# Half loads completed by ScalarE copies, two shifts replaced by loads, and the products for M placed earlier in a fused CIN kernel

## The chip, the cores and the metric

The kernel runs on one core of a Trainium2 chip. The metric is the device time of one execution in microseconds (us), lower is better; where a profile is shown, its times count from the start of the profiled span. The engines are called PE (TensorE), ACT (ScalarE), DVE (VectorE), POOL (GpSimd) and SP (SyncE, which here only issues DMAs); PEld is PE's loading of weights.

## The reference

The reference is a three-layer "compressed interaction network" on `x` of shape (1024, 64, 16): batch, fields, embedding. Each layer multiplies every field of `x` with every field of the last hidden state, elementwise over the embedding, and contracts the 64 x 64 products with a weight matrix of 128 rows.

```python
x0 = x; h = x; xs = []
for i in range(3):
    z = jnp.einsum('bfe,bge->bfge', x0, h)          # all pairs of fields
    z = z.reshape(Bn, f0 * fh, e)
    y = jnp.einsum('oc,bce->boe', Ws[i], z) + bs[i][None, :, None]
    if i != 2: x_i, h = y[:, :64], y[:, 64:]         # half goes out, half goes on
    else:      x_i, h = y, y
    xs.append(x_i)
pooled = jnp.sum(jnp.concatenate(xs, axis=1), axis=2)
return pooled @ fc_w.T + fc_b                        # (1024, 1)
```

All data are float32. Since the result is one number per batch row, the last layer's weights can be folded with `fc_w` into one 64 x 64 x 64 form, called M in this text, that acts on pairs of hidden and input fields.

## The kernel before, in words

The batch is cut into 32 chunks of 32 rows; a chunk is a matrix of 64 fields by N = 512 columns. The products of all field pairs are symmetric, so the kernel forms 16 blocks per chunk, `t = 4*j + i`. Block (j, i) multiplies a copy of x whose rows are rotated by i with a copy rotated by 4(j + 1), and by 16 more in the upper 64 partitions. The first copy is the tile `xa`, of 128 partitions by 4 x 512; its upper 64 partitions hold the same values as its lower 64, since the host array `xra` repeats x's rows with period 64. The second copy is made of four quarters `xb[c][j]` of 128 x 512. `product(c, j)` (line 242) multiplies a whole `xa` with one quarter into a block buffer `z` of 128 x 2048, on DVE by default, on POOL where `engine=nc.gpsimd` says so. `half_contract(c, j)` (line 252) contracts the four blocks of one j on PE into the accumulator `acc`: eight matmuls, two for each block. `w_all` holds the weights; `h1_weights(j)` (line 302) makes its left half from the loaded `w0t` with the help of a copy by ACT (lines 312 and 321 to 326).

This work concerns the head of the kernel, about the first 57 us, in which the first four chunks `c0, c1, c2, c3` (`HEAD`, chunks 2, 3, 0, 1) go through the first layer while the weights for the rest are made. Its order is written out by hand: each engine runs its instructions in the order in which the code names them, and waits at each for its operands and for its output buffer.

- Loads, all on SP's queue, in this order: first row block of c0's `xa`, the first quarter of w0 (`wh`), c0's other blocks, c1's first block, the rest of w0 (`w0r`), the rest of c1's `xa`, w2 in two parts, w1, then c2's `xa` and its four quarters. c3 follows after c0's last product, in c0's `xa` buffer.
- The quarters of c0 and c1 are not loaded. PE makes them out of `xa` with a shift matrix (`shift_pair`, line 221), into PSUM banks. One of each chunk is copied to SBUF by ACT (lines 314 and 339), because POOL multiplies with it.
- Quarters of c2 and c3 are loaded. Where POOL works at the same time, ACT copies a quarter into a PSUM bank first, and DVE reads it there (lines 397 and 429).
- M: `pv` (line 359) on PE, two transposes (line 364) and two small copies (line 371) on DVE, two small copies on ACT (line 372), which together give the weights `v2t`; then `pm` (line 386) on PE, its evacuation by ACT (line 400), a write to memory (lines 415 to 421) and skewed reads back (lines 459 and 465), from which DVE makes the right half of `w_all` (line 495).
- After c3 PE runs the second half of the head's contractions with that right half (`head_q_tile`, line 270); then the steady loop begins, whose instructions are sorted by due times written by hand (line 526 is its matmul helper, lines 634 and 651 its products and sums, line 554 its copies into PSUM).

PSUM tiles come from three tags: `acc` with four banks, `y` and `set` with two each. A tile of a tag waits until the tile that had its bank before is done with. The pool of `xa` has three buffers, that of `xb` nine.

Of the kernel before, what the change touches and what calls it, by code (L numbers as in the profile page):

```python
# [37 lines left out]
F32 = mybir.dt.float32  # L38
# [4 lines left out]
F = 64  # L43
# [3 lines left out]
N = CB * E  # L47
# [3 lines left out]
NI = 4  # L51
NJ = 4
NT = NI * NJ
XR = 128 + NI
# [16 lines left out]
def cin_kernel(ctx, tc, xra, xrb, wh, w0r, w1h, w2t, wx1, wx0, vec, out):  # L71
    nc = tc.nc
    ctx.enter_context(tc.manual_schedule())
    const = ctx.enter_context(tc.tile_pool(name="const", bufs=1))
    xp = ctx.enter_context(tc.tile_pool(name="xp", bufs=3))
    sp = ctx.enter_context(tc.tile_pool(name="sp", bufs=2))
    ps = ctx.enter_context(tc.tile_pool(name="ps", bufs=2, space=bass.MemoryType.PSUM))
    dr = ctx.enter_context(tc.tile_pool(name="dr", bufs=1, space=bass.MemoryType.DRAM))
    halves = [slice(0, F), slice(F, 128)]

    def const_tile(name, shape):
        return const.tile(shape, F32, tag=name, name=name)
# [4 lines left out]
    def take(uses=1):  # L87
        n = vacant.pop(0)
        left[n] = uses
        return n  # L90

    def used(n, times=1):
        left[n] -= times
        assert left[n] >= 0
        if left[n] == 0:
            vacant.append(n)
# [22 lines left out]
    for base in (0, 64, -64):  # L119
        nc.gpsimd.affine_select(  # L120
            out=shift, in_=shift, compare_op=ALU.not_equal, fill=1.0, base=base,
# [19 lines left out]
    xas, xbs, xxs, es = {}, {}, {}, {}  # L141

    def load_xa(c, at=slice(0, NI)):
        if c not in xas or at.start == 0:
            xas[c] = xp.tile([128, NI, N], F32, tag="xa", name=f"xa_{c}")
        nc.sync.dma_start(  # L146
            out=xas[c][:, at, :],
            in_=bass.AP(
                tensor=xra.tensor, offset=c * XR * N + at.start * N,
                ap=[[N, 128], [1, (at.stop - at.start) * N]],  # L150
            ),
        )

    def quarter(c, j):
        xbs.setdefault(c, {})[j] = xp.tile([128, N], F32, tag="xb", name=f"xb_{c}_{j}", bufs=9)
        return xbs[c][j]

    def load_xb(c, *js):
        for j in js or range(NJ):
            nc.sync.dma_start(out=quarter(c, j), in_=xrb[c, :, j, :])  # L160
# [22 lines left out]
    def load_chunk(c):  # L183
        load_xa(c)
        load_xb(c)

    c0, c1, c2, c3 = HEAD
# [5 lines left out]
    w1s = flat(w1b)  # L193
    load_xa(c0, slice(0, 1))
    nc.sync.dma_start(out=w0t[:, 0, :], in_=wh)
    load_xa(c0, slice(1, 2))
    load_xa(c0, slice(2, 4))
    load_xa(c1, slice(0, 1))
    nc.sync.dma_start(out=w0t[:, 1:NJ, :], in_=w0r)
    load_xa(c1, slice(1, 4))  # L200
    w0s = [w0t[:, j, :].rearrange("p (i v g) -> p i v g", v=2, g=F) for j in range(NJ)]
    xb_gps = [quarter("gps", n) for n in range(2)]
    for k in range(2):
        nc.sync.dma_start(out=w2s[k], in_=w2t[k])
    nc.sync.dma_start(out=w1s, in_=w1h)
    load_xa(c2)
    load_xb(c2)


# [2 lines left out]
    def shifted(c, j, tag):  # L212
        xbs.setdefault(c, {})[j] = ps.tile(
            [128, N], F32, tag=tag, name=f"xp_{c}_{j}", bufs=4 if tag == "acc" else 2
        )

    def shift_pair(c, js):
        for r, j in enumerate(js):
            for h in range(2):
                at = 4 * (j + 1) + 16 * h  # L220
                nc.tensor.matmul(  # L221
                    xbs[c][j][halves[h]], shift[halves[r], at : at + F],
                    xas[c][halves[r], 0, :], start=True, stop=True,
                )
# [6 lines left out]
    acc = const_tile("acc", [128, 2, NCH // 2, CB])  # L231
# [3 lines left out]
    def new_acc(c, n=N, tag="acc"):  # L235
        accs[c] = ps.tile([128, n], F32, tag=tag, name=f"acc_{c}", bufs=4 if tag == "acc" else 2)

    def product(c, j, first=0, last=NI, engine=nc.vector, uses=1):
        if first == 0:
            zs[c, j] = take(uses)  # L240
        at = slice(first, last)
        engine.tensor_tensor(  # L242
            blocks[zs[c, j]][:, at, :], xas[c][:, at, :],
            xbs[c][j].unsqueeze(1).to_broadcast([128, last - first, N]), ALU.mult,
        )

    def half_contract(c, *js, last=None):
        for j in js:
            for i in range(NI):
                t = j * NI + i  # L250
                for n in range(2):
                    nc.tensor.matmul(  # L252
                        accs[c][halves[n]], w_all[:, t, 0:64],
                        blocks[zs[c, j]][:, i, n * H2 : (n + 1) * H2],
                        start=(t == 0), stop=(j == last and i == NI - 1),
                    )
            used(zs[c, j])

    def keep_h1(c):
        for n in range(2):  # L260
            nc.scalar.activation(
                hb[halves[c % 2], c // 2, n * H2 : (n + 1) * H2], accs[c][halves[n]],
                AF.Identity, bias=bh1[halves[n]],
            )
# [36 lines left out]
    def h1_weights(j, other=None):  # L301
        nc.vector.tensor_tensor(
            w_all[:, j * NI : (j + 1) * NI, 0:64], w0s[j][:, :, 0, :],
            w0s[j][:, :, 1, :] if other is None else other, ALU.add,
        )
# [5 lines left out]
    w0o = [w0p[:, 0], w0p[:, 1], w0q[:, 0], w0q[:, 1]]  # L311
    nc.scalar.copy(w0o[0], w0s[0][:, :, 1, :])
    h1_weights(0, w0o[0])
    nc.scalar.copy(xb_gps[0], xbs[c0][1])
    xbs[c0][1] = xb_gps[0]
    for i in ((0, 2), (2, 3), (3, 4)):
        product(c0, 1, *i, engine=nc.gpsimd)
    product(c0, 0, 0, 1)
    product(c0, 0, 1, 2)
    product(c0, 0, 2, NI)  # L320
    nc.scalar.copy(w0o[1], w0s[1][:, :, 1, :])
    product(c0, 2, 0, 2)
    h1_weights(1, w0o[1])
# [6 lines left out]
    half_contract(c0, 0)  # L330


    for j, tag in ((0, "y"), (3, "acc"), (1, "y"), (2, "set")):
        shifted(c1, j, tag)
    shift_pair(c1, (0, 3))
    half_contract(c0, 1)
    shift_pair(c1, (1, 2))
    new_acc(c1, H2)
    nc.scalar.copy(xb_gps[1], xbs[c1][3])
    xbs[c1][3] = xb_gps[1]  # L340

    product(c0, 3)
    load_chunk(c3)
    half_contract(c0, 2, 3, last=3)
    keep_h1(c0)


    for j in range(NJ - 1):
        product(c1, j)
    product(c1, NJ - 1, engine=nc.gpsimd)  # L350

# [17 lines left out]
    for h in range(2):  # L369
        at = slice(32 * h, 32 * h + 32)  # L370
        nc.vector.tensor_copy(v2t[halves[h], at], v2q[halves[h]])
        nc.scalar.copy(v2t[halves[1 - h], at], v2q[halves[h]])
    used(v2b)
    half_contract(c1, 0, 3, 1)


    mb = take()
# [15 lines left out]
    pcx = ps.tile([128, 1], F32, tag="acc", name="pcx", bufs=4)  # L393
    for to in halves:
        nc.tensor.matmul(pcx[to], v2t[0:64], bh2, start=True, stop=True)
    xb2 = ps.tile([128, N], F32, tag="set", name=f"xp_{c2}_{NJ - 1}")
    nc.scalar.copy(xb2, xbs[c2][NJ - 1])
    xbs[c2][NJ - 1] = xb2
    for m in (0, 2, 1, 3):
        nc.scalar.copy(m_sb[:, m, :], pms[m])  # L400

    half_contract(c1, 2, last=2)

# [3 lines left out]
    def m_ap(f1, f2, dims):  # L409
        return bass.AP(tensor=md.tensor, offset=md.offset + f1 * row + f2 * F, ap=dims)  # L410
# [3 lines left out]
    for half, queue in enumerate((nc.sync, nc.scalar)):  # L414
        queue.dma_start(
            out=m_ap(0, 32 * half, [[row, F], [1, 32 * F]]), in_=m_rows[halves[half]]
# [5 lines left out]
        out=m_ap(64, 68, [[row, 4], [4 * F, 7], [1, 4 * F]]),  # L422
        in_=m_rows[0:4, 4 * F :].rearrange("p (k c) -> p k c", c=4 * F),
    )
    used(mb)

    for j in (0, 1):
        xb3 = ps.tile([128, N], F32, tag="y", name=f"xp_{c3}_{j}")
        nc.scalar.copy(xb3, xbs[c3][j])
        xbs[c3][j] = xb3  # L430
    nc.scalar.activation(cx, pcx, AF.Identity, scale=1.0 / QS)
    keep_h1(c1)
    for c in KEPT:
        copy_x(c)

# [567 lines left out]
    last = cuts[1]  # L1003
# [84 lines left out]
```

## Time and profile before

| | us |
|---|---|
| median of 3 runs | 452.6 (452.0 to 452.67) |
| the profiled execution, its own time | 453.01 |
| its span in the profile | 451.2 |
| PE busy in the span | 445.1 |
| DVE busy | 393.1 |
| POOL busy | 364.4 |
| ACT busy | 116.8 |

The times of the stages named in the text come from the profiled execution. A busy share is a mean over stages: which engine matters in a stage is read from who waits for whom there. In the listings of groups and of the timeline a line reads: start and length in us (or count and mean), engine, source line, operation, output from input with sizes, and in brackets the idle time before it and what ended it. Matmuls of float32 leave two records each, so eight matmuls appear as x16.

### The profile page before, as it was taken

The numbers are of one execution on the slowest core, as the hardware profiler recorded it, in microseconds if no ns is written. First come the engines' busy times: TensorE is split into PE (matmuls) and PEld (weight loads), VectorE is DVE, ScalarE is ACT, GpSimd is POOL, SyncE is SP. The second block draws the span as 40 slices with busy tenths as digits, with TensorE's granted clock in tenths as the row PEclk, the third lists the DMA queues.
The fourth block names the chain that finished last, engine by engine and source line by source line (L and its number), as shares of the span: only waits on it lengthen the run. The fifth ranks groups of instructions, "written<-read, shape, count | busy, mean of one in ns | idle before, by whom it ended". The sixth has DMA issues, their size and how long they took to land.

```text
span 451.2 us, 6067 instructions
## 1 busy us (share of the span) xinstructions
PE 445.1 (99%) x2302; PEld 178.9 (40%) x2302; DVE 393.1 (87%) x284; ACT 116.8 (26%) x215; POOL 364.4 (81%) x125
## 2 busy tenths in 40 slices
PE   7999999999999999999999999999999999999997
PEld 4565343442334433343333433344333433344435
DVE  3996598998989998999999899999989999998734
ACT  2163241323312213231221313131131313114111
POOL 5413687999996979899797979979797997979900
PEclk9999999999999999999999999999999999999999
DMA  8996999395949386694958769493967949591500
GB/s 297 415 306 157 322 393 359 114 336 155 324 114 333 121 226 256 133 360 105 281 179 230 259 153 336 107 319 135 252 238 161 341 105 314 176 270 44 107 0 2
DMA packets 34484, 99.67 MB, mean 221 GB/s; under 512 B 6324, under 2 KB 6996, under 8 KB 27864
## 3 DMA queue, kind: packets, MB, share of 16 engines
q1 hardware_dynamic: 31800, 84.70, 52.5%
q0 software_dynamic: 1872, 13.63, 16.9%
q10 hardware_dynamic: 784, 0.95, 0.8%
q8 instruction: 18, 0.29, 0.3%
q14 instruction: 10, 0.08, 0.0%
HBM read 84.00 MB, written 1.64 MB: 190 GB/s over the span
## 4 chain that ended last, share of the span: by engine, by line
PE 96%; DMA 2%; POOL 1%; SPq 0%; issue 0%; DVE 0%; ACT 0%; POOLq 0%; ACTq 0%
PE alpha L526 45%; PE delta L526 20%; PE beta L526 10%; PE acc L526 6%; PE acc L252 6%; PE q L526 3%; PE acc L270 3%; DMA z<-in_w0r 2%; POOL z L651 1%; PE y L526 0%; PE pm L386 0%; PE pv L359 0%; SPq L146 0%; PE xp L221 0%; PE hx L526 0%
## 5 line engine op out<-in xcount | busy, mean ns | idle before, releaser
L651 POOL TENSOR_TENSOR z<-z,z 128x2048 f32<-128x2048 f32 (+1 forms) x78 | 299.6, 3874 | 29.2 <-PE alpha L526 29.1
L634 DVE TENSOR_TENSOR z<-xa,xp 128x2048 f32<-128x2048 f32 x103 | 231.7, 2279 | 2.6 <-issue 1.4
L526 PE MATMUL alpha<-z,ws 128*64 128x512 f32 x624 | 222.1, 593 | 0.0
L526 PEld LDWEIGHTS alpha<-z,ws 128*64 128x64 f32 x624 | 71.7, 137 | 86.3 <-issue 85.5
L526 PE MATMUL delta<-z,w_all 128*64 128x512 f32 x208 | 95.6, 593 | 0.7 <-POOL z L651 0.7
L554 ACT COPY xp<-xb 128x512 f32<-128x512 f32 x88 | 51.6, 588 | 169.5 <-DVE z L634 141.6
L526 PE MATMUL beta<-z,w_all 128*64 128x512 f32 x208 | 93.8, 595 | 0.0
L526 PE MATMUL alpha<-z,w_all 128*64 128x512 f32 x208 | 92.0, 595 | 0.0
L526 PE MATMUL delta<-z,ws 128*64 128x512 f32 x208 | 91.6, 593 | 0.0
L242 DVE TENSOR_TENSOR z<-xa,xp 128x2048 f32<-128x2048 f32 (+2 forms) x23 | 45.0, 2002 | 6.3 <-ACT xp L554 4.8
L242 POOL TENSOR_TENSOR z<-xa,xb 128x2048 f32<-128x2048 f32 x6 | 27.5, 4646 | 19.6 <-DMA xb<-in_xrb 19.6
L526 PEld LDWEIGHTS delta<-z,w_all 128*64 128x64 f32 x208 | 28.3, 137 | 32.9 <-issue 30.4
L526 PEld LDWEIGHTS alpha<-z,w_all 128*64 128x64 f32 x208 | 27.5, 137 | 29.9 <-issue 24.0
L526 PEld LDWEIGHTS delta<-z,ws 128*64 128x64 f32 x208 | 28.1, 137 | 23.7 <-issue 22.8
L526 PEld LDWEIGHTS beta<-z,w_all 128*64 128x64 f32 x208 | 26.9, 137 | 24.2 <-issue 23.0
L252 PE MATMUL acc<-z,w_all 128*64 128x256 f32 x256 | 29.1, 382 | 2.3 <-DVE z L242 2.0
L526 PE MATMUL acc<-z,w_all 128*64 128x512 f32 (+1 forms) x96 | 29.7, 594 | 0.0
L252 PEld LDWEIGHTS acc<-z,w_all 128*64 128x64 f32 x256 | 18.0, 137 | 14.6 <-DVE z L242 3.8
L665 ACT ACTIVATE snap<-alpha,vs 64x512 f32<-64x512 f32 x13 | 8.9, 684 | 54.8 <-PE alpha L526 54.8
L294 DVE TENSOR_REDUCE acc<-uu 128x64 f32<-128x1024 f32 (+2 forms) x19 | 19.6, 1036 | 0.2
L682 DVE SCALAR_TENSOR_TENSOR uu<-alpha,snap 64x512 f32<-64x512 f32 x13 | 9.0, 689 | 12.2 <-PE alpha L526 12.2
L662 ACT COPY snap<-alpha 64x512 f32<-64x512 f32 x13 | 7.6, 581 | 46.2 <-PE alpha L526 29.7
(117 smaller groups left out, 356.4 us busy)
## 6 DMA issues: line engine op xcount, KB each, us to landing
xa<-in_xra SPq DMA_DIRECT2D x32, 1024.0 KB, 8.5
xb<-in_xrb SPq DMA_DIRECT2D x128, 256.0 KB, 8.0
z<-z POOLq DMA_DIRECT2D x13, 1024.0 KB, 8.5
e<-in_xra SPq DMA_DIRECT2D x28, 128.0 KB, 7.3
xx<-in_xra SPq DMA_DIRECT2D x28, 128.0 KB, 2.5
z<-in_w2t SPq DMA_DIRECT2D x2, 1024.0 KB
z<-in_wx SPq DMA_DIRECT2D x2, 1024.0 KB, 10.0
z<-in_w1h SPq DMA_DIRECT2D x1, 1024.0 KB
```

Of the source, the lines that this page charges most:

```text
L242: engine.tensor_tensor(blocks[zs[c, j]][:, at, :], xas[c][:, at, :], xbs[c][j].unsqueeze(1).to_broadcast([128, last - first, N]), ALU.mult,)
L252: nc.tensor.matmul(accs[c][halves[n]], w_all[:, t, 0:64], blocks[zs[c, j]][:, i, n * H2 : (n + 1) * H2], start=(t == 0), stop=(j == last a ...
L270: nc.tensor.matmul(accs[c][halves[1 - c % 2]], w_all[:, t, 64:128], blocks[zs[c, j]][:, i, :], start=(t == 0), stop=False, skip_group_chec ...
L294: nc.vector.tensor_reduce(acc[rows, of, k, half], uu[rows, of if at is None else at, E * half.start : E * half.stop].rearrange("p k (b e) ...
L526: nc.tensor.matmul(out, w, rhs, start=start, stop=stop, skip_group_check=True)
L554: nc.scalar.copy(bank, xbs[c][j])
L634: engine.tensor_tensor(blocks[b], xas[c], xbs[c][j].unsqueeze(1).to_broadcast([128, NI, N]), ALU.mult)
L651: nc.gpsimd.tensor_tensor(*(blocks[b][:, first:last] for b in (o, x, y)), ALU.subtract if in1 == "T3" else ALU.add,)
L662: nc.scalar.copy(snaps[0][p["O"]], alpha(p))
L665: nc.scalar.activation(snaps[1][p["O"]], alpha(p), AF.Identity, bias=bh1[p["A"]])
L682: nc.vector.scalar_tensor_tensor(uu[p[out], 0], x(p), 1.0 / QS, factor[p[out]], ALU.mult, ALU.mult)
```

## The change

`load_half` loads only the lower 64 partitions of an `xa`, and `copy_half` lets ACT copy them to the upper 64. c0's blocks 1 to 3, c1's blocks 1 to 3, and all of c2 and c3 are loaded in this way; the first blocks of c0 and c1 are still loaded whole. Quarters 1 and 2 of c1 are loaded behind c1's `xa` and copied by ACT into the PSUM banks that PE's second pair of shifts filled. The product (c1, 2) moves behind the transposes and copies of M's weights on DVE, and the group (c1, 1) moves behind the products for M on PE, so that two of c1's four groups lie on each side of `pm`. Quarter 1 of c2 is copied to a PSUM bank in place of quarter 3, and quarters 2 and 3 of c2 are copied too, after the evacuation of M. On ACT the copy of c2 stands behind `keep_h1(c0)` and ahead of the small copies of `v2t`; the copy of c3 stands behind the copies of c2's quarters.

```diff
+    def load_half(c, at=slice(0, NI)):
+        if at.start == 0:
+            xas[c] = xp.tile([128, NI, N], F32, tag="xa", name=f"xa_{c}")
+        nc.sync.dma_start(
+            out=xas[c][halves[0], at, :],
+            in_=bass.AP(
+                tensor=xra.tensor, offset=c * XR * N + at.start * N,
+                ap=[[N, F], [1, (at.stop - at.start) * N]],
+            ),
+        )
+
+    def copy_half(c, at=slice(0, NI)):
+        nc.scalar.copy(xas[c][halves[1], at, :], xas[c][halves[0], at, :])
...
     load_xa(c0, slice(0, 1))
     nc.sync.dma_start(out=w0t[:, 0, :], in_=wh)
-    load_xa(c0, slice(1, 2))
-    load_xa(c0, slice(2, 4))
+    load_half(c0, slice(1, 2))
+    load_half(c0, slice(2, 4))
     load_xa(c1, slice(0, 1))
     nc.sync.dma_start(out=w0t[:, 1:NJ, :], in_=w0r)
-    load_xa(c1, slice(1, 4))
+    load_half(c1, slice(1, 4))
...
+    load_xb(c1, 1, 2)
     for k in range(2):
         nc.sync.dma_start(out=w2s[k], in_=w2t[k])
     nc.sync.dma_start(out=w1s, in_=w1h)
-    load_xa(c2)
+    load_half(c2)
     load_xb(c2)
...
     h1_weights(0, w0o[0])
+    copy_half(c0, slice(1, 2))
     nc.scalar.copy(xb_gps[0], xbs[c0][1])
+    for i in (2, 3):
+        copy_half(c0, slice(i, i + 1))
...
-    product(c0, 0, 0, 1)
-    product(c0, 0, 1, 2)
-    product(c0, 0, 2, NI)
+    for i in range(NI):
+        product(c0, 0, i, i + 1)
...
-    for j, tag in ((0, "y"), (3, "acc"), (1, "y"), (2, "set")):
+    loaded = [xbs[c1][j] for j in (1, 2)]
+    for j, tag in ((0, "y"), (3, "acc"), (1, "y"), (2, "acc")):
         shifted(c1, j, tag)
     shift_pair(c1, (0, 3))
     half_contract(c0, 1)
-    shift_pair(c1, (1, 2))
     new_acc(c1, H2)
     nc.scalar.copy(xb_gps[1], xbs[c1][3])
     xbs[c1][3] = xb_gps[1]
+    copy_half(c1, slice(1, 4))
+    for j in (1, 2):
+        nc.scalar.copy(xbs[c1][j], loaded[j - 1])
 
     product(c0, 3)
-    load_chunk(c3)
+    load_half(c3)
+    load_xb(c3)
     half_contract(c0, 2, 3, last=3)
     keep_h1(c0)
-
-
-    for j in range(NJ - 1):
+    copy_half(c2)
+
+
+    for j in range(NJ - 2):
         product(c1, j)
     product(c1, NJ - 1, engine=nc.gpsimd)
...
     used(v2b)
-    half_contract(c1, 0, 3, 1)
+    product(c1, NJ - 2)
+    half_contract(c1, 0, 3)
...
-    xb2 = ps.tile([128, N], F32, tag="set", name=f"xp_{c2}_{NJ - 1}")
-    nc.scalar.copy(xb2, xbs[c2][NJ - 1])
-    xbs[c2][NJ - 1] = xb2
+    def banked(c, j, tag):
+        bank = ps.tile([128, N], F32, tag=tag, name=f"xp_{c}_{j}")
+        nc.scalar.copy(bank, xbs[c][j])
+        xbs[c][j] = bank
+
+    banked(c2, 1, "set")
     for m in (0, 2, 1, 3):
         nc.scalar.copy(m_sb[:, m, :], pms[m])
 
-    half_contract(c1, 2, last=2)
+    half_contract(c1, 1, 2, last=2)
...
+    for j in (2, 3):
+        banked(c2, j, "y")
+    copy_half(c3)
+    keep_h1(c1)
     for j in (0, 1):
-        xb3 = ps.tile([128, N], F32, tag="y", name=f"xp_{c3}_{j}")
-        nc.scalar.copy(xb3, xbs[c3][j])
-        xbs[c3][j] = xb3
+        banked(c3, j, "y")
     nc.scalar.activation(cx, pcx, AF.Identity, scale=1.0 / QS)
-    keep_h1(c1)
```

## The prediction

> **What bounds the kernel now.** I read the page first. TensorE (PE) is busy for almost the whole span:
>
> ```profile
> PE 445.1 (99%) x2302; PEld 178.9 (40%) x2302; DVE 393.1 (87%) x284; ACT 116.8 (26%) x215; POOL 364.4 (81%) x125
> ```
>
> So a change in the first 45 us moves the end only by what it does to PE's queue. I therefore read the chain of waits for 0 to 60 us (start, length, what):
>
> ```profile
> 3.10 7.41 DMA z<-in_w0r
> ...
> 11.56 1.95 PE acc L252 x16
> 13.51 1.02 PE xp L221 x8
> 14.53 3.60 PE acc L252 x32
> 18.13 1.85 PE pv L359 x16
> 19.98 5.33 PE acc L252 x48
> 25.32 1.86 PE pm L386 x14
> ...
> 27.25 15.69 PE acc L252 x144
> ```
>
> The reader sees that the load of w0r holds PE until 11.56, and that from there PE never stops: one block's group is 15.69/9 = 1.74 us, the second pair of shifts 1.02, M's products (pm) stand at 25.32, and the last group of c3 ends at 42.94. Next I asked for PE's idle time; after 11.56 the only entry is
>
> ```profile
> 107.17 0.64 PE L526 MATMUL delta<-z,w_all 128*64 128x512 f32 x1 [0.72 <-POOL z L651]
> ```
>
> PE is 0.72 us early there, so a delay of PE alone loses 0.72 on the way, and a gain of PE alone is worth nothing unless POOL moves too.
>
> Then ACT's timeline, since the change gives ACT more to do, in order of its queue:
>
> ```profile
> 18.18 0.96 ACT L261 ACTIVATE hb<-acc,vs 64x256 f32<-64x256 f32 x2 [5.99 <-PE acc L252]
> 23.25 0.50 ACT L372 COPY res<-z 64x32 f32<-64x32 f32 x2 [4.12 <-DVE z L364]
> 26.42 0.59 ACT L397 COPY xp<-xb 128x512 f32<-128x512 f32 x1 [2.66 <-PE pm L386]
> ```
>
> Line 372 makes half of pm's weights. It ends at 23.75, 1.5 us ahead of pm. Last, the SP queue's waits and issues between 21.6 and 25 us:
>
> ```profile
> SPq L160 <- DMA xa<-in_xra: 2.2, 1, 2.2
> ```
> ```profile
> 23.74 1.02 SPq L160 DMA_DIRECT2D xb<-in_xrb  x2
> ```
>
> SP's n-th load goes out when load n-8 has landed (7.98 fits c0's last piece, 10.52 w0r, 12.40 c1's last piece). So this wait dates a landing: c2's x is there at about 23.7.
>
> **What the Trainium skill says.** "ScalarE: Activation LUTs", What ACT_TABLE_LOAD costs: 186 ns + 0.833 ns per element with immediates, 612 ns for 512; the trace has 613 to 618 for 64x512, so it agrees, and I estimate 1.47 us for c1's copy (1536) and 1.89 for c2's or c3's (2048). "PSUM — Partial Sum Buffer", Engine vs sequencer instructions: ScalarE's queue is strict FIFO; the trace agrees (every ACT line stands in program order). "SBUF — State Buffer", Door 1: a load to partitions 0..63 reaches half of the ports, 196 GB/s at 1 MiB against 328. The trace agrees only in part. Windows with e and xx loads alone (64 partitions) against full loads (last columns: DMA share, GB/s):
>
> ```profile
> 85.70:88.10 2.40, 2.40 (x13) 1.44 (x12) 2.37 (x5) 0.41 (x1) 2.40 (x1) 1.00 0.77 212
> 127.80:128.70 0.90, 0.90 (x7) 0.29 (x4) 0.90 (x2) 0.44 (x1) 0.90 (x1) 1.00 0.40 146
> 129.30:130.50 1.20, 1.20 (x8) 0.43 (x6) 1.17 (x2) 0.13 (x1) 1.20 (x1) 1.00 0.67 207
> 12.00:18.00 6.00, 6.00 (x54) 3.28 (x50) 6.00 (x6) 0.19 (x1) 4.57 (x1) 1.00 1.01 422
> ```
>
> Per unit of share, half loads run at 275, 365 and 309 GB/s, full ones at 418. They are slower per byte, but not by two. I take 309; ends 418 (no loss) and 218 (the page's limit of 8 ports).
>
> **The change, part by part.**
> (1) Loads. Halved: 0.79 MB of c0, 0.79 of c1, 1.05 of c2 (2.62 MB, 6.27 us at 418). The halves are 1.31 MB, 4.24 us at 309: 2.03 saved. Added: c1's two quarters, 0.52 MB, 1.25 us, ahead of w2, w1 and c2. So c2's x lands 0.78 earlier, at 22.9; ends 21.8 (418) and 24.7 (218). c3 gains later, with its cover unchanged (POOL's wait for it ended at 31.6, and its product is wanted after 37). SP gets two more issues of about 0.4 us; its queue is not what limits here.
> (2) The head. w0r lands 0.6 earlier (1.88 for 0.79 MB becomes 1.27), at 9.9; c0's last piece at 7.3 instead of 7.95. Now c0's blocks 1 to 3 wait for ACT copies of 0.61, the last until 8.6; then DVE's 0.68 + 1.2, and the weight sum of 0.42 ends at 10.9. PE goes on at 10.95 instead of 11.56. POOL's first product starts near 6.85 instead of 5.89, since its operand's copy stands behind c0's; it ends at 11.7, and PE wants its last block at 12.2.
> (3) Two shifts gone: PE -1.02. Their places are filled by two ACT copies of 0.59, done by about 14.5; DVE wants them at 15.0 and 17.2. c1's copy (1.47) ends near 13.2; POOL's product of c1 then runs 13.2 to 17.8 (12.54 to 17.1 before), wanted at about 20.3.
> (4) Order. PE now runs c0's other groups, pv and two groups of c1 before pm: 10.95 + 1.95 + 3.60 + 1.85 + 3.55, with 0.3 for c0's last product, is 22.2. DVE's transposes and copies for pm, moved ahead of c1's third product, end near 21.1. So far this gains 3.1 us on pm.
> (5) **The added wait that decides.** c2's copy is put into ACT's queue ahead of line 372. It starts when c2's x lands, 22.9 + 0.05, takes 1.89, and only then come line 372's 0.50 and 0.05 to PE: pm at 25.4. Behind pm on PE stand c1's last two groups and all of c2 and c3. PE stands still from 22.2 to 25.4, and everything that (2) to (4) earned is spent.
> (6) After pm PE has the 17.62 that it had (25.32 to 42.94) and one group more, 1.74: c3 ends at 25.4 + 19.36 = 44.77, **1.83 later**. DVE is not the bound there: c2's first product starts at 24.9, the third waits for its PSUM copy behind the evacuation of pm (30.5), the last of c3 ends at 41.7; PE wants it at 43.0. ACT's copy of c3 and the two for c3's quarters, which wait for c2's products in their buffers, fit in between.
> (7) M's round trip through memory starts with pm: 25.4 against 25.32, so +0.1. The loads of the next chunks, issued behind it, and POOL's queue up to 107.1 follow it. PE's +1.83 less the 0.72 there is +1.1. If the wx loads, whose buffers PE frees at about 62 us, carry PE's delay to POOL, the full 1.83 remains. I take +1.3. After 107 the order is unchanged and costs nothing more.
>
> **Sum.** In numbers, with L for c2's landing: change = L - 21.8 (between that and 0.7 more). The profiled execution has a span of 451.2 and a time of 453.01; +1.3 gives 454.3. It lies 0.4 above the median of the three runs, 452.6, so I predict 453.9.
>
> **Rivals.**
> **A, the forecast** (L from 22.2 to 23.7): +0.4 to +2.6, 453.0 to 455.2. Chance 0.55, of which 0.10 falls within 0.9 us. For it: the order in ACT's queue is certain, the landing is dated by SP's wait.
> **B, half loads at the port limit** (L about 24.7): pm at 27.2, c3's end +3.6, M's trip +1.9; 455.5 to 456.2. PE would idle for 5 us, and "TensorE: Matmul & The Clock Gate", Part 1, halves the clock after an idle window of 3.4 us; no stretch of this trace past 11 us has such a gap, so I price it between 0 and 1.7 more. For it: the page; against: the 275 to 365 GB/s per unit of share above. Chance 0.15.
> **C, faster: c2 lands before 21.** w2's second part lands at 17.4 (SP's issue at 17.37), w1 only at 21.17, 3.8 us for 1.05 MB while the DMA moved over 400 GB/s: some DMA engine lags behind by 1.3. If the new order does not meet that lag and half loads cost no more per byte, L is 20.5, pm 23.0, c3's end 42.35 (-0.6), and with POOL's start 2.4 earlier the 0.72 is won too: -1.3, 451.3. It decides where L falls under 21.8, or under 20.9 for a gain beyond 0.9 us. Chance 0.17, of which 0.03 within.
> **D, nothing to see:** L between 21.4 and 22.2, head gain and stall cancel: 452.2 to 453.0. Chance 0.13, of which 0.12 within 0.2%, 0.01 faster.
>
> **How the numbers follow.** 0.2% is 0.9 us, about what a measurement of this kernel can tell from no change. Faster: 0.14 + 0.01 = 0.15. Within: 0.10 + 0.03 + 0.12 = 0.25. Slower: 0.45 + 0.15 = 0.60. The range 451.8 to 455.8 leaves out most of C's best end and half of B. A's own range is 453.0 to 455.2.
>
> **What would show it.** In the changed profile: pm on PE preceded by an idle 2 to 4 us put down to ACT line 372 (or its new number); the copy of c2 on ACT, about 1.9 us, starting at c2's landing between 22 and 24 us; PE leaving w0r's wait near 11; two shifts of c1 instead of four; c3's last group ending near 44.8. Wrong: PE running through from 11 to 42 without that gap; a c2 copy that starts before 21; half loads with a share per byte as of full ones.

## The result and the profile after

The changed kernel takes 458.64 us (median of 6 runs, 457.55 to 461.12) against 452.31 (6 runs, 451.91 to 453.53) for the kernel before on the same chip. The ratio is 1.014, with a 95% interval of 1.0111 to 1.0169: slower by 6.3 us. The profiled execution took 459.13. Its page begins:

```profile
span 457.3 us, 6072 instructions
...
PE 446.1 (98%) x2294; PEld 176.5 (39%) x2294; DVE 392.4 (86%) x285; ACT 126.0 (28%) x225; POOL 364.5 (80%) x125
```

The span grew by 6.1 us and PE's busy time by 1.0, although the two shifts (1.02) are gone from it. So about 5 us of the loss are PE standing still; the rest, and what the shifts had given, went into slower work of PE. The busy shares of the other engines hardly moved and say nothing of the cause. The chain of waits of the changed kernel names it (start, length, what; its last pieces in this stretch):

```profile
7.85 18.64 DMA xa<-in_xra
...
26.50 1.19 ACT xa L166
27.69 0.62 issue
28.31 0.24 ACT res L394
...
28.56 0.25 ACT res L394
...
28.85 3.28 PE pm L409 x14
32.13 0.13 PE pcx L418 x3
32.26 17.65 PE acc L267 x160
```

Read from the bottom: the first layer's remaining ten groups start at 32.26, right behind `pm`. `pm` starts at 28.85, right behind ACT's two small copies (line 394, which was 372). These stand behind ACT's copy of c2, and that one behind the load of c2's half, which landed at 26.5. The piece of 18.64 us is not one slow transfer: it begins with c2's place in the line of loads, behind everything that was issued before. PE's timeline, with the idle time before a group in brackets, shows the same stall from PE's side:

```profile
8.66 1.25 PE L267 MATMUL acc<-z,w_all 128*64 128x256 f32 x8 [0.87 <-DVE z L257]
...
13.18 3.67 PE L267 MATMUL acc<-z,w_all 128*64 128x256 f32 x32 [2.25 <-DVE w_all L317]
17.08 1.95 PE L267 MATMUL acc<-z,w_all 128*64 128x256 f32 x16 [0.23 <-DVE z L257]
...
28.85 3.31 PE L409 MATMUL pm<-z,res 64*64 64x512 f32 x16 [4.32 <-ACT res L394]
```

There is a second thing in the last line: `pm` itself took 3.3 us, where it took 1.86 before. The windows of the changed kernel show why (stretch, its length, then busy time and instructions of PE, PEld, DVE, ACT, POOL; the last three columns are the granted TensorE clock, the DMA share and GB/s):

```profile
9.20:13.00 3.80, 1.73 (x14) 0.41 (x12) 1.52 (x3) 0.76 (x3) 2.73 (x3) 1.00 1.01 183
13.50:21.00 7.50, 7.28 (x66) 3.88 (x64) 7.50 (x6) 3.82 (x6) 4.56 (x1) 1.00 1.03 422
21.20:26.00 4.80, 3.33 (x32) 1.94 (x28) 4.10 (x6) 0.00 (x0) 0.00 (x0) 1.00 0.99 188
27.60:32.00 4.40, 3.15 (x19) 1.07 (x20) 3.57 (x2) 2.85 (x6) 0.00 (x0) 0.69 1.00 188
...
24.50:26.00 1.50, 0.04 (x2) 0.00 (x0) 0.90 (x1) 0.00 (x0) 0.00 (x0) 1.00 0.99 202
26.00:27.50 1.50, 0.00 (x0) 0.00 (x0) 0.00 (x0) 0.99 (x1) 0.00 (x0) 1.00 1.12 396
29.40:32.60 3.20, 3.20 (x22) 1.30 (x16) 3.20 (x2) 1.51 (x4) 0.00 (x0) 0.50 0.98 208
```

The DMA share is 1.0 in the first four, so transfers are queued up all the time. In the stretches in which the half loads of c1 (first window), c2 (third) and c3 (fourth) move, 183 to 188 GB/s get through; in the second, in which nearly all is w2 and w1, for all partitions, 422. The slow stretches are mixed: quarters for all partitions move in them as well. The fifth window shows this at its clearest. These are its transfers:

```profile
DMA packets 166, 0.30 MB, mean 202 GB/s; under 512 B 21, under 2 KB 21, under 8 KB 165
```

A row of a half load of c2 has 8 KB, a row of a quarter 2 KB; the 21 packets under 512 B carry next to nothing. So all but one of the 145 rows in this window belong to quarters, and they too move at half the rate; 396 GB/s are reached only from 26.0 on. In the kernel before, where every load is whole, a stretch with 459 such rows (20.0 to 23.7) moved at 396. So the half loads seem to slow down what is queued with them. The last window is the slow `pm`: the granted clock is 0.50.

**The account.** c3's last group ends at 32.26 + 17.65 = 49.91, against 42.94 before: +6.97. `pm` starts 3.53 later, takes 1.42 longer, and has 2.02 more behind it: 1.74 for the one group that moved there, and 0.28, about what the low clock costs there, since it lasts until 32.7. At 107 us PE no longer waits for POOL, which takes the 0.72 of before off: +6.25, beside a span that grew by 6.1.

### The profile page after: what moved, and what is told of

Read it like the earlier page. It is cut to its first block, busy times and chain, and to the rows that moved or that the text cites. A ratio compares the mean times of both kernels' runs of the same rounds, so it can differ in the third digit from the quotient of the medians.

```text
span 457.3 us, 6072 instructions
## 1 busy us (share of the span) xinstructions
PE 446.1 (98%) x2294; PEld 176.5 (39%) x2294; DVE 392.4 (86%) x285; ACT 126.0 (28%) x225; POOL 364.5 (80%) x125
## 4 chain that ended last, share of the span: by engine, by line
PE 93%; DMA 5%; SPq 0%; ACT 0%; issue 0%; DVE 0%
PE alpha L553 45%; PE delta L553 18%; PE beta L553 11%; PE acc L553 6%; DMA xa<-in_xra 5%; PE acc L267 4%; PE q L553 3%; PE acc L285 3%; PE pm L409 1%; PE y L553 0%; ACT xa L166 0%; PE hx L553 0%; SPq L157 0%; SPq L220 0%; PE pc L917 0%
## 5 line engine op out<-in xcount | busy, mean ns | idle before, releaser
L257 DVE TENSOR_TENSOR z<-xa,xp 128x2048 f32<-128x2048 f32 (+2 forms) x26 | 49.6, 1953 | 8.4 <-ACT xp L581 5.7
```

The costliest lines, as they stand in the source:

```text
L257: engine.tensor_tensor(blocks[zs[c, j]][:, at, :], xas[c][:, at, :], xbs[c][j].unsqueeze(1).to_broadcast([128, last - first, N]), ALU.mult,)
```

## The experiments

**Theory:** a half load takes about as long as a whole one, so that c2's x lands some 4 us later than forecast; ACT's queue carries that to `pm`, and the long idle time lowers the clock. **Rivals:** the place of c2's copy in ACT's queue alone; the loads for the two shifts, which stand ahead of w2, w1 and c2; the moved order around M; a slow DMA queue that a second queue would mend. Each ratio below is against runs of the kernel before on the same chip, with its 95% interval.

**1. c2 loaded whole.** The changed kernel with one load undone:

```diff
-    load_half(c2)
+    load_xa(c2)
...
-    copy_half(c2)
```

> The kernel after, with c2's x loaded whole and its copy on ACT left out; c0, c1 and c3 stay half loads. Theory (the copy of c2 holds ACT's queue until c2's half load lands at 26.5 us, and the two small copies behind it hold the products for M on PE): ACT is free at 22.7, so M's products start at about 24.5, when PE comes to them, without the idle 4.3 us and at full clock; then c2's products on DVE, from about 27, set the end of c3's groups near 44.1 instead of 49.9, and the time is about 453 us, 5 to 6 below the kernel after. Rival (c2's x is late whatever stands on ACT, because the quarters of c1 and the half loads of c0 and c1 delay it): little changes, 456 to 458 us.

Measured: 454.45 against 452.82, ratio 1.004 (1.0019 to 1.006). PE's timeline and, after it, the SP issue that waits for c2's x:

```profile
24.07 1.95 PE L408 MATMUL pm<-z,res 64*64 64x512 f32 x16
...
40.97 5.40 PE L267 MATMUL acc<-z,w_all 128*64 128x256 f32 x48 [2.10 <-POOL z L257]
```
```profile
24.43 1.00 SPq L174 DMA_DIRECT2D xb<-in_xrb  x2
```

`pm` now follows without idle time and takes 1.95. This one half load, with its copy, carries 1.0 of the 1.4%, 4.5 us. And the whole c2, twice the bytes, landed at 24.4 in this execution, 2 us *earlier* than its half in that of the changed kernel. What is left is a wait of 2.1 for POOL's product of c3, whose x is still a half load with a copy.

**2. c2's copy moved behind the small copies of M's weights**, loads as in the changed kernel:

```diff
     keep_h1(c0)
-    copy_half(c2)
...
     used(v2b)
+    copy_half(c2)
     product(c1, NJ - 2)
```

> The kernel after with one line moved: on ACT the copy of c2's x stands behind the two small copies for M's weights instead of ahead of them; all loads as in the kernel after. Theory: M's products start near 24.5 at full clock; c2's x still lands at 26.5 and its copy still ends at 28.4, so DVE's products of c2 start at 28.4 as before and set the end of c3's groups at 28.4 + 15.5 + 1.75 = 45.7 instead of 49.9: about 454.3 to 455.1 us. Rival (the lateness of c2's x costs it all, its place in the queue nothing): no change, 458.6 us.

Measured: 455.36 against 452.82, ratio 1.0063 (1.004 to 1.0086).

```profile
24.73 1.95 PE L409 MATMUL pm<-z,res 64*64 64x512 f32 x16
...
30.90 0.44 PE L267 MATMUL acc<-z,w_all 128*64 128x256 f32 x2 [0.56 <-DVE z L257]
```

The stall ahead of `pm` is gone, as is the low clock, though c2's half landed as late as ever (its copy starts at 26.62). But the delay only changes its place: DVE's products of c2 cannot start before 28.55, and PE then waits 0.25 to 0.56 for each of the next groups; c3 ends at about 46.7. The queue place decides where the late load hurts and about half of how much (0.63% is left of 1.4%), not whether.

**3. Every load whole.** All `load_half` become `load_xa` and all `copy_half` go; the loads in place of shifts and the order around M stay.

> The kernel after with every x loaded to all 128 partitions as in the kernel before and all copies of halves left out; the two loads in place of PE's shifts and the new order of M's products stay. Theory (half loads save no time, so giving them up costs none): c2's x lands at about 25.0, later than before by the 1.25 us of the two added quarters, M's products start near 22.5, DVE's products of c2 start near 25.7 and c3's groups end at about 42.9: 451.5 to 452.5 us. Rival (the added quarters are what delays the head): 455 us or more.

Measured: 453.49 against 452.82, ratio 1.0025 (1.0013 to 1.0037). Two lines of PE's timeline:

```profile
19.71 1.07 PE L376 MATMUL pv<-z,fv 128*32 128x512 f32 x8 [1.16 <-DMA z<-in_w2t]
...
24.31 1.95 PE L404 MATMUL pm<-z,res 64*64 64x512 f32 x16
```

Against the kernel of experiment 1 the half loads of c0, c1 and c3 together are worth 0.15% (1.004 less 1.0025), with intervals that overlap. With none left the kernel is still 0.25% or 1.1 us slower than before, which I had not expected. The trace shows why the quarters' loads bring no gain: they put w2 off, and `pv` waits 1.16 for it, as much as the two shifts had cost (1.02). It doesn't show where the 1.1 us go, since the profiled execution (452.99) is as fast as that of the kernel before (453.01); this stays open.

**4. The order around M alone**, on the kernel before:

```diff
-    for j in range(NJ - 1):
+    for j in range(NJ - 2):
...
-    half_contract(c1, 0, 3, 1)
+    product(c1, NJ - 2)
+    half_contract(c1, 0, 3)
...
-    half_contract(c1, 2, last=2)
+    half_contract(c1, 1, 2, last=2)
```

> The kernel before with the new place of M's products alone: the third product of c1 behind M's transposes on DVE, and c1's groups 0 and 3 before, 1 and 2 behind M's products on PE. All loads, shifts and copies are those of before. Theory: M's products start at 23.5 instead of 25.3, M's trip and the loads behind it start 1.8 earlier, PE's sum is the same, and at most the 0.72 us that PE waits for POOL at 107 is won: 451.9 to 452.6 us against 452.6. Rival (POOL's queue there hangs on later loads): no change.

Measured: 452.29 against 452.67, ratio 0.9999 (0.9985 to 1.0012).

```profile
23.74 1.95 PE L387 MATMUL pm<-z,res 64*64 64x512 f32 x16
...
25.67 17.49 PE L252 MATMUL acc<-z,w_all 128*64 128x256 f32 x160
```

`pm` starts at 23.74 rather than 25.32, and c3 still ends at about 43.0, since PE has the same work and no idle time either way. PE no longer waits for POOL at 107 us in this trace, but the 0.72 does not show in the ratio. An earlier M is worth nothing measurable.

**5. The loads by themselves.** Behind the last work of the kernel before, three loads each of an `xa` to all partitions, to 0..63, to 64..127, to every second partition (64 of them), and to 0..31. A small copy on DVE behind each (`mark`) dates its landing:

```diff
+    for n, rows in enumerate((
+        slice(0, 128), slice(0, 64), slice(64, 128), slice(0, 128, 2), slice(0, 32),
+    )):
+        for m in range(3):
+            load_rows(m, rows, 3 * n + m)
+        for m in range(3):
+            nc.vector.tensor_copy(mark[:, 3 * n + m : 3 * n + m + 1], flat(m)[:, 0:1])
```

> The kernel before, with loads by themselves behind its last work, in five groups of three, each load of 8 KB rows: 128 partitions (1 MB), partitions 0 to 63, partitions 64 to 127, 64 partitions at every second place (0, 2, ... 126), partitions 0 to 31. Nothing reads what they bring, and nothing else runs beside them. Theory (a load to one half of the partitions uses half of the ports into SBUF): about 418 GB/s for the first group, 180 to 220 for the second, third and fifth, and 400 or so for the fourth, whose rows lie on all ports. Rival (64 rows are slow for their number): the fourth runs at 180 to 220 as well. Rival of the prediction (half loads lose little per byte): 300 or more for the second and third.

Windows over the first four groups (the columns are those of above):

```profile
452.00:458.50 6.50, 0.00 (x0) 0.00 (x0) 0.31 (x2) 0.00 (x0) 0.00 (x0) 0.56 1.00 413
460.00:466.00 6.00, 0.00 (x0) 0.00 (x0) 0.46 (x3) 0.00 (x0) 0.00 (x0) 0.50 0.99 202
467.00:473.00 6.00, 0.00 (x0) 0.00 (x0) 0.46 (x3) 0.00 (x0) 0.00 (x0) 0.50 1.02 209
474.00:476.00 2.00, 0.00 (x0) 0.00 (x0) 0.15 (x1) 0.00 (x0) 0.00 (x0) 0.50 0.99 406
```

Between one landing and the next lie 2.69 and 3.02 us for a whole tile, 2.40 to 2.50 for the lower half, 2.33 to 2.52 for the upper, and 1.25, 1.22 and 1.81 for 64 partitions taken every second (the transfers paused before the last of these). So half of a tile takes nearly as long as the whole, and it is not the number of partitions that matters but which. This fits what the Trainium skill states in "SBUF — State Buffer", Door 1 (the DMA port swizzle): partitions 0..63 reach 8 of the 16 ports. It gives 196 GB/s at 1 MiB; measured are 202 here, and 209 for the upper half. The fifth group, 32 partitions, ran out too soon to be read (178 GB/s at a DMA share of 0.73).

**6. The change with its ports mended:** the halves of c0, c1 and c2 go to every second partition, behind a zeroing of the tile by DVE or POOL.

```diff
+        if c in HEAD[:3]:
+            (nc.gpsimd if c == HEAD[2] else nc.vector).memset(xas[c][:, at, :], 0.0)
...
-            out=xas[c][halves[0], at, :],
+            out=xas[c][slice(0, 128, 2) if c in HEAD[:3] else halves[0], at, :],
```

> The kernel after, with the half loads of c0, c1 and c2 put on every second partition (0, 2, ... 126) instead of partitions 0 to 63: same bytes, same number of rows, same copies on ACT, same order. Both halves are zeroed ahead of the loads by DVE and POOL while these are idle, and what the copies move is then not x, so the results are not the reference's: its time alone is of use. Theory (a load to partitions 0 to 63 is held by its ports): c0's and c1's loads gain 1.15 us each and c2's 1.5, so that c2 lands at 22.7, M's products start at 25.1 after an idle time under 3 us and at full clock, c3's groups end at 44.5: 453.7 to 454.5 us. This is also what the prediction's sum gives where a half load costs half. Rival (64 rows or the added copies are the cost): 457 to 459 us.

Measured: 453.08 against 452.67, ratio 1.0006 (0.9995 to 1.0018). ACT's and then PE's timeline, and the window ahead of c2's landing:

```profile
21.08 1.90 ACT L168 COPY xa<-xa 64x2048 f32<-64x2048 f32 x1 [3.70 <-DMA xa<-in_xra]
```
```profile
23.43 1.95 PE L411 MATMUL pm<-z,res 64*64 64x512 f32 x16 [1.40 <-ACT res L396]
```
```profile
18.00:21.10 3.10, 3.10 (x30) 1.87 (x28) 3.00 (x6) 0.02 (x1) 0.00 (x0) 1.00 1.00 399
```

The same bytes, the same copies and the same queues, and c2 is there when its copy starts, at 21.1 instead of 26.5, earlier than I had expected (22.7). Of 1.4%, 0.06% is left, so which partitions the halves go to decides nearly all of the loss (c3's half is still on partitions 0..63 here). The run also suggests what the change could have been worth: with half loads at the full rate it stands level with the kernel before. The kernel leaves out the copies that would put x's rows in place for the products; what these would cost was not measured.

**7. The queue place alone.** The kernel before, with ACT work of c2's copy's kind, waiting for c2's load, at the place of that copy:

```diff
     keep_h1(c0)
+    for n in range(2):
+        nc.scalar.copy(uu[halves[0]], xas[c2][halves[0], 2 * n : 2 * n + 2, :])
```

> The kernel before with one thing added: at the place in ACT's queue where the kernel after copies c2's x, two copies of c2's lower half into a tile that is not in use yet (2.0 us together); all loads are whole and nothing reads the copies. Theory (the place in the queue is a wait of its own): ACT stands until c2 lands at 23.7, M's products start at 26.3 instead of 25.3, c3's groups end at 43.9, and M's trip through memory is later by as much: about 453.8 us, 1 more than before. Rival (ACT has room for it): no change.

Measured: 453.38 against 452.67, ratio 1.0015 (1.0005 to 1.0026).

```profile
26.65 1.95 PE L388 MATMUL pm<-z,res 64*64 64x512 f32 x16 [1.00 <-ACT res L374]
```

The added wait is real, but with c2 loaded whole it costs 1.00 of PE's time and 0.7 us of the whole. The rival that lays all on the queue place is out.

**8 and 9. PE kept busy in the stall.** Matmuls with zero weights ahead of `pm`, whose result is overwritten; they change no wait, only whether PE stands still. The second kernel has four where the first has nine:

```diff
+    for _ in range(9):
+        nc.tensor.matmul(pms[0], zeros, xas[c1][:, 0, :], start=True, stop=True)
     for m in (0, 1):
```

> The kernel after with nine matmuls of 128x512 by a zero weight ahead of M's products on PE, which write the bank that M's first product overwrites. They take 9 x 0.43 = 3.9 us and lie in the 4.3 us in which PE stood still. Theory (the idle time brought PE's clock down, so that M's products took 3.3 us instead of 1.95): M's products still start at 28.85 but take 1.95, and the time falls by 1.3 to about 457.3. Rival (M's products are slow for another reason, such as w1's late landing): 3.3 us again, 458.6 us.

The first was mis-sized. One such matmul took 0.89 us, not 0.43, and nine ran past the point at which `pm` could start: 461.59 against 452.67, ratio 1.0192 (1.0162 to 1.0223).

```profile
25.16 7.99 PE L407 MATMUL pm<-xa,const-float32-0.0 128*128 128x512 f32 x18
33.08 1.95 PE L411 MATMUL pm<-z,res 64*64 64x512 f32 x16
```

Its time tells nothing of the clock's worth, but its last line does show `pm` back at 1.95. With four:

> The kernel after with four matmuls of 128x512 by a zero weight ahead of M's products, 4 x 0.89 = 3.55 us by the length that they had with nine, so that they end before M's weights are ready. Theory (the idle time brought PE's clock down): M's products start when they did, about 2.4 us after c2's landing, take 1.95 instead of 3.3, and the time falls by 1.3 to about 457.3. Rival (no clock effect): 3.3 us again, 458.6.

Measured: 456.3 against 452.57, ratio 1.0081 (1.0057 to 1.0105).

```profile
23.89 3.70 PE L407 MATMUL pm<-xa,const-float32-0.0 128*128 128x512 f32 x8
28.03 1.95 PE L411 MATMUL pm<-z,res 64*64 64x512 f32 x16 [0.44 <-ACT res L394]
```

With useless work added the kernel is 0.6% faster (1.0081 for 1.014), more than expected. `pm` is 1.4 shorter, which is the clock. Its start is 0.8 earlier, since c2 landed at 25.7 in this execution and not at 26.5. The added matmuls are not the cause of that: PE had come out of its wait for w0r 0.86 earlier already (12.32 for 13.18), ahead of all of them. Why is not settled.

**10. c0 and c1 whole, c2 and c3 half:** `load_half` becomes `load_xa` for the first two chunks, and their copies go.

> The kernel after with c0's and c1's x loaded whole as before and their copies on ACT left out; c2 and c3 stay half loads with their copies in the same place. Theory (a half load takes as long as a whole one): c2 lands where it did or up to 0.5 us earlier, and the time is 457.5 to 458.7. Rival (the prediction's price, 0.6 us saved on each of c0 and c1): c2 lands 1.2 later, 459.8 us.

Measured: 459.92 against 452.57, ratio 1.0168 (1.0144 to 1.0192).

```profile
11.53 3.67 PE L267 MATMUL acc<-z,w_all 128*64 128x256 f32 x32 [0.55 <-DVE w_all L317]
...
29.43 3.69 PE L405 MATMUL pm<-z,res 64*64 64x512 f32 x16 [5.22 <-ACT res L390]
```

The head is better, since w0r is there 1.7 earlier (ACT's copy of it starts at 10.55 instead of 12.21): PE goes on at 11.53 instead of 13.18. It buys nothing, since PE then waits for c2, which landed at 27.1. The ratio lies above that of the whole change, with intervals that overlap, and nearer to the value expected by the rival. I do not lean on that: c2 landed anywhere from 25.7 to 28.7 in the kernels with its half load behind the same queue. Whether the halves of c0 and c1 save a few tenths stays open.

**11. The two shifts back on PE**, without the loads in their place:

```diff
-    load_xb(c1, 1, 2)
...
+    shift_pair(c1, (1, 2))
...
-    for j in (1, 2):
-        nc.scalar.copy(xbs[c1][j], loaded[j - 1])
```

> The kernel after with PE's second pair of shifts for c1 back, and c1's two added quarters and their copies left out. Theory (loads are served in order, and c2 stands behind the quarters): c2 lands 1.25 us earlier, at about 25.2, PE comes to M's products 1.0 later, so it is idle for only about 2 us and keeps its clock, M's products start at 27.7, c3's groups end near 47.1: 456 to 456.6 us. Rival (the quarters cost nothing, the shifts cost PE 1.0): 458.6 to 459.6.

Measured: 457.74 against 452.57, ratio 1.0136 (1.0099 to 1.0172). ACT's timeline, then PE's:

```profile
24.84 1.90 ACT L166 COPY xa<-xa 64x2048 f32<-64x2048 f32 x1 [5.95 <-DMA xa<-in_xra]
```
```profile
27.19 3.41 PE L406 MATMUL pm<-z,res 64*64 64x512 f32 x16 [3.85 <-ACT res L391]
```

With 0.52 MB less ahead of it c2's half lands 1.65 earlier (1.25 was expected), and ahead of every landing seen with them (25.7 to 28.7); so the quarters' loads seem to have pushed it back, though this is one execution. The time did not follow as far as expected (457.7 for 456 to 456.6): the idle time is still 3.85, and the slow `pm`, which I had expected to go, is still there.

**12. Would a second queue help?** Loads by themselves again, in pairs to partitions 0..31 and 64..95, which by the page named in experiment 5 reach different ports; first both from SP's queue, then one from ACT's:

```diff
+    quarters_ = (slice(0, 32), slice(64, 96))
+    for n, queues_ in enumerate(((nc.sync, nc.sync), (nc.sync, nc.scalar))):
+        for m in range(3):
+            for queue, rows in zip(queues_, quarters_):
+                load_rows(queue, m, rows, 3 * n + m)
```

> The kernel before, with loads by themselves behind its last work: three pairs of loads of 8 KB rows, one to partitions 0 to 31 and one to partitions 64 to 95, first with both loads of a pair on SP's queue, then with one on SP's and one on ACT's. Nothing reads what they bring. Theory (each such load reaches half of the ports, and one queue is served in order): 210 to 220 GB/s for pairs on one queue; with two queues the two halves run side by side and reach 380 or more. Rival (the queues are served in turn and each load still has all engines on its half): about 220 GB/s for both.

The two windows:

```profile
451.50:456.50 5.00, 0.00 (x0) 0.00 (x0) 0.31 (x2) 0.00 (x0) 0.00 (x0) 0.55 1.02 246
457.00:463.00 6.00, 0.00 (x0) 0.00 (x0) 0.46 (x3) 0.00 (x0) 0.00 (x0) 0.50 1.03 239
```

239 GB/s from two queues, 246 from one: no gain, and the rival was right. That is far from the 413 of whole tiles and agrees with the Trainium skill, "SBUF — State Buffer", "Can I just issue two DMAs to hit both halves?", which finds two transfers, to partition 0 and partition 64, nearly in series (+6%). What helped here is one transfer whose own partitions are spread over both halves, as in experiment 6.

## Why the prediction was wrong in size

The direction and the mechanism of the forecast were right: c2's copy, ahead of the small copies in ACT's queue, held `pm` up. The size was not: 458.6, against 453.9 with a range up to 455.8. Step by step:

**Step 1, the price of a half load, is the one that failed.** It took 309 GB/s, out of 275, 365 and 309 worked out as GB/s over DMA share. That division is not allowed. The windows it came from had moved 212, 146 and 207 GB/s and never more. A share below 1 there meant that little was queued, not that the same stream would run faster with more. Nor were all their loads of the kind to be priced: those of `xx` come in pairs, one to each half of the partitions (line 169). With a share of 1.0 such loads moved 202 alone (experiment 5), and the stretches with them in the changed head 183 to 188. At 188 the 1.31 MB of halves take 6.97 us instead of 4.24: an estimate of 2.7 out of the 3.6 by which c2 landed late (26.5 for 22.9), and only an estimate, since other loads share these stretches. The rest may lie in the slowing of those other loads, in the order of the queue and in the scatter of that landing, which I could not separate. The page quoted had nearly the right value, 196 GB/s at 1 MiB; the prediction used the page's limit of 218, and only as an end with a chance of 0.15. Experiments 5 and 6 show that the halving holds here, alone and in the kernel.

**Step 2** had c0's halves right: the last of them was there at 7.24, as forecast (7.3). But w0r did not land 0.6 earlier, at 9.9, but near 12.2 (ACT waited for it until 12.21), 1.7 later than before. So it was not held up by what stood ahead of it alone: its last rows came in the stretch of 183 GB/s, among c1's half and c1's two quarters, which were issued behind it. With both of these in the queue w0r's copy on ACT started between 11.34 and 12.74 in five executions (the change, experiments 1, 2, 8 and 9); without the quarters at 10.34 (experiment 11), with c0 and c1 whole at 10.55 (experiment 10), and with the halves on every second partition at 9.19 (experiment 6). How a later load comes to delay an earlier one, no run shows. PE went on at 13.18 instead of 10.95. POOL's first product started at 7.11, close to the 6.85 expected.

**Step 3.** The shifts' 1.02 went, and the copies took what was estimated, as ACT's timeline shows:

```profile
12.21 0.38 ACT L338 COPY w0p<-z 128x256 f32<-128x256 f32 x1 [3.80 <-DMA z<-in_w0r]
...
13.93 1.47 ACT L166 COPY xa<-xa 64x1536 f32<-64x1536 f32 x1
...
26.50 1.90 ACT L166 COPY xa<-xa 64x2048 f32<-64x2048 f32 x1 [6.48 <-DMA xa<-in_xra]
28.31 0.49 ACT L394 COPY res<-z 64x32 f32<-64x32 f32 x2
```

1.47 and 1.90 us agree with the Trainium skill, "ScalarE: Activation LUTs", What ACT_TABLE_LOAD costs, from which 1.47 and 1.89 were worked out. Both came later than forecast: c1's because ACT waited for w0r until 12.21 ahead of it, c2's because of its own load.

**Step 4.** PE came to `pm` at 24.5, not 22.2, from the late w0r. This cost nothing more: PE would have waited for c2 in any case.

**Step 5** named the right wait. From the landing on, its sum holds: 26.5 + 1.9 + 0.5 + 0.05 is 28.95, and `pm` started at 28.85. The last two lines above are that wait.

**Step 6** left out the clock. c3's end came 5.14 later than its 44.77: 3.45 from the start of `pm` (28.85 for 25.4), 1.42 from the slow `pm`, and 0.28 behind it, where the clock was still low. The clock had been priced, at 0 to 1.7, but only in rival B, on the strength of the Trainium skill, "TensorE: Matmul & The Clock Gate", Part 1, which puts the idle window at about 3.4 us. The lengths of `pm` agree: after 1.0 and 1.4 us of idle time (experiments 7 and 6) it took 1.95; after 3.85, 4.32 and 5.22 (experiments 11, the change, 10) it took 3.41, 3.31 and 3.69; and with PE kept busy, 1.95. After the 2.25 of idle time ahead of 13.18 the clock was still 1.00. The delay is not a fixed one, though: the granted clock fell to 0.50 at 26.8, 29.3 and 26.5 in these three, which is 3.4, 4.8 and only 2.3 us after PE had stopped. In the change the low clock cost 1.4 us in `pm` and about 0.3 behind it, and this counts in full on the path.

**Step 7.** The gain of 0.72 at 107 was lost, as said. M's trip, taken as 0.1 late, began 3.5 late with `pm`; PE's own delay covered it.

The formula, change = L - 21.8 to 0.7 more, was good as far as its input went: with the measured landing, 26.5, it gives 4.7 to 5.4, and with the clock's 1.4 and 0.3 it gives 6.4 to 7.1, against 6.3 measured. Its lower end is the one in which the 0.72 at 107 is taken off, as it was. Its gain side is untested: with L at 21.1 it gives -0.7 to 0.0, and experiment 6 measured -0.2 to 0.8 us.

**The rivals.** B is the one that came closest: it named the half loads' limit and the clock. But its landing (24.7) was still too early, since its rate of 218 was above the 188 that the queue reached, and its times, 455.5 to 456.2 with up to 1.7 for the clock, ended below the 458.6. C and D fell with the landing; and C's gain is not there even where its condition comes close: experiments 4 and 6 show that neither an earlier M nor a c2 at 21.1 brings a measurable one. None of the kernels run here measurably beats the kernel before.

## What to carry to other kernels

Price a DMA that reaches few partitions by the rate that such transfers reached while nothing else moved, never by a rate divided by a share of less than one. Halving the bytes of a load by dropping partitions 64 to 127 saved little time by itself (2.40 to 2.50 us for 2.69) and cost some among other loads; taking every second partition halved the time. Before an instruction that waits for a transfer is put into an in-order queue, look at what stands behind it, and if PE at the end of that chain would idle for some 4 us, as here, count its slow restart too.

## What the runs showed of the hardware that I had not expected

- Half loads cost more among others than alone, and the others are slow beside them: 183 to 188 GB/s in the head's backlog, 202 and 209 by themselves, and 202 in a stretch in which all but one of the rows belonged to quarters for all partitions. In the head, c2's half landed 2 us later than the whole c2 in its place (26.5 and 24.4, one execution each).
- 64 partitions taken every second reach 406 GB/s, as much as all 128 (413), and 399 in the head.
- Once down, the granted clock stayed at 0.50 for about 3.4 us in the change (29.3 to 32.7) and in experiment 11 (26.8 to 30.2), and for about 6.8 in experiment 10 (26.5 to 33.3).
- A float32 matmul of 128x512 took 0.89 us with 128 columns of weights (nine in 7.99). The 0.43 that I had taken is the time from one record to the next where there are 64 columns; there two matmuls run side by side (at 99.49 and 99.55, then again at 99.92 and 99.98 in the kernel before), and each leaves two records.
- With the same loads ahead of it, c2's half landed at 25.7, 26.5, 26.6 and 28.7 in four kernels. The copy of w0r had started in the same order, at 11.34, 12.21, 12.22 and 12.74, so the scatter begins early in the head. No run explains it.
